# Layer 0's value sums in eights, a fourth weight buffer, and an earlier end of a pass, in a two-layer attention and expert kernel

## Chip, core and metric

The kernel runs on one core of a Trainium2 chip, in one launch. The metric is the device time of that core in microseconds (us). Engines are named as the profile names them: PE is the matrix engine (TensorE), PEld its weight loads, DVE the vector engine, ACT the scalar engine, POOL is GpSimd, and SP only issues transfers. PSUM is the memory that PE writes its results to, SBUF the working memory.

## What is computed

There are 16 sequences of 512 tokens with 128 features, all float32, and two layers. What matters here is cut out of the reference:

```python
# both layers, 16 heads of 8 features, B = 16 sequences, S = 512 tokens
scores = einsum('bhqd,bhkd->bhqk', q, k) / sqrt(8)      # layer 1: causal, keys after the query at -inf
attn   = softmax(scores, axis=-1)
ctx    = einsum('bhqk,bhkd->bhqd', attn, v)

# layer 0: x + memory(xn) + block(xn)
#   memory: a test-time-trained two-layer MLP, updated by gradient steps over 8 chunks of 64 tokens (a scan)
#   block:  convolution, attention as above once, layernorm, 8 dense experts of width 512, layernorm
# layer 1: x + attn1(xn) + moe(xn)
#   attn1:  q,k,v; causal attention; a convolution of its result gives new queries; causal attention
#           again with the same k,v
#   moe:    a router takes 8 of 32 experts a token (128 places each), small MLPs, weighted sum
```

So each sequence has one attention without a mask in layer 0 and two causal ones in layer 1.

## The kernel before

**Turns.** Everything is written as Python generators ("stages") that the class `Turns` steps in turns: in every turn each live stage is stepped once, in the order of its priority number, and what it emits goes into the program. PE executes in exactly this order (it is under a manual schedule), so the order of stages in a turn is the order of PE's work. The other engines' orders are made by the framework's scheduler, in part bound by `issue_after`. A stage that is added to `turns.stages` with the current turn's number joins in the next turn.

**One attention pass.** The 16 heads are done in two halves (c = 0 and 1), a pass each. A pass has two parts. `largest` (priority 0) computes scores and takes row maxima on DVE; `weighted` (priority 1) later computes the transposed scores again with the maxima folded in, 64 rows deep in two halves of the array (float32r), takes the exponential on ACT into a tile `e` (L470), and multiplies `e` with the values into PSUM tile `pc` (L196, 128 rows deep, 32 columns wide, four heads beside each other in the array). One step of `weighted` is called a look; one turn has at most one look of `largest` and one of `weighted`. In layer 0 a pass has 16 looks of two heads over 512 queries. In layer 1 the mask cuts it to 11: four looks 512 wide, four 384 wide, two 256 wide (four heads each), and one 128 wide with eight heads. There POOL zeroes the masked triangle of `e` with two selects per look (L474), after the exponential and before the value product.

**The value products lag.** Finished heads wait in a list `old`. In a later look, behind that look's scores on PE, `tail(pools["heads"])` sums heads in groups of four, at most two groups at once, and only if the list holds at least `pools["heads"]`. That number is 4 in the first part of the program and 8 from the start of layer 1's work on. What is left at the end of a pass is done by the stage `summed` (priority 2): value products, the copy `cs` of `pc` to SBUF on ACT (L444), a transpose `tpc`, and the division by the softmax sums on DVE.

```python
        locks.remove("p2")
        free_slots.append(slot)
        turns.stages.append((turns.turn, 2, ends(summed(old, tail, last, c, cnv), name)))
```

These lines (L484 to L486) run when `weighted` is stepped once more after its last look, in the turn after it; `summed` itself is first stepped one turn later still. The lock `p2` lets the next pass take its first look in the turn in which it is removed. PSUM holds one score tile of `weighted` at a time (`p2` = 1), so a look's scores wait for the exponential of the look before.

**Buffers.** `e` takes 4 KB of each partition. In the first part all `e` tiles come from three buffers of pool `att`; later they come alternately from three of `att` and three of `mid`. Pool `sm` keeps four buffers of each of its small tiles.

**Around it.** The memory scan (priority 3) shares the first part with layer 0's attention. The dense experts of layer 0, `ffn` (priority 6, PE matmuls `phe` and `pye`, L584 and L594), run as a filler of turns: a balance of estimated PE time decides how many units each turn gets, and with `pools["pairs"]` none go into a turn with value products unless more than three are due. `middle` (priority 4) ends layer 0 and computes layer 1's router: logits `lg`, their eight largest, a mask `lr`, and weights that go with the tokens into `xwt` and to memory. `fill` adds a matmul without use to a turn with little work for the array while the experts do not run.

Of the kernel before, what the change touches and what calls it, by code (L numbers as in the profile page):

```python
# [9 lines left out]
F32 = mybir.dt.float32  # L10
# [4 lines left out]
ALU = mybir.AluOpType  # L15
AX = mybir.AxisListType

P = 128
B, S, D = 16, 512, 128
N = B * S  # L20
TB = S // P
# [6 lines left out]
NT8, NH = 8, 4  # L28
EXP0, DFF = 8, 512

EXP1, FF1, TOPK = 32, 96, 8
# [42 lines left out]
def bc(ap, axis, n):  # L74

    u = ap.unsqueeze(axis)
    shape = list(u.shape)
    shape[axis] = n
    return u.to_broadcast(shape)
# [3 lines left out]
def network(ctx: ExitStack, tc: tile.TileContext, a, out):  # L83
    nc = tc.nc
# [4 lines left out]
    sm = ctx.enter_context(tc.tile_pool(name="sm", bufs=4))  # L89
# [50 lines left out]
    pools, done, locks, clock, newest, cleared, held, read, cell = {}, {}, set(), [0], [None], [None], [0], [0], []  # L140
# [3 lines left out]
    def mark(*m):  # L144
        done[m] = clock[0]
# [27 lines left out]
    def drop():  # L173

        read[0] += 1
# [89 lines left out]
    def ends(stage, name):  # L265
        yield from stage
        mark(*name)
# [155 lines left out]
    def weighted(slot, vp, c, causal, cn, name):  # L423


        q, k, _ = slot
        yield from acquire("p2")
        cnv = cn.rearrange("p t (a c j d) -> p (t a) c j d", c=2, j=2, d=DH)
        old, last = [], []
        got = []  # L430

        def values(heads):
            for head in heads:
                kt, n, t, r, e = head
                lent.discard(id(head))
                g = 2 * (t % 2) + r
                j = t // 2
                mm(
                    got[0][32 * g : 32 * g + 32, S - n :], vp[:, kt, 4 * g + 2 * c + j, :], e,
                    start=(kt == 0 and j == 0), stop=(kt == TB - 1 and j == 1),  # L440
                )
            if kt == TB - 1 and t == NH - 1:
                cs = att.tile([P, S], F32, tag="cs", bufs=1, name="cs")
                nc.scalar.copy(cs, got[0])  # L444
                locks.remove("ctx")
                last.append(cs)

        def tail(least):
            if not got and "ctx" not in locks:
                locks.add("ctx")  # L450
                got.append(pools["ps"].tile([P, 512], F32, tag="ctx", bufs=1, name="pc"))
            if got and len(old) >= least:
                locks.add("values")
                for _ in range(min(len(old) // 4, 2)):
                    values([old.pop(0) for _ in range(4)])

        for i, (kt, n, per, t) in enumerate(widths(causal)):
            while len(old) >= pools["heads"] and not got and "ctx" in locks:
                yield
            s = pools["ps"].tile([P, 2, 512], F32, tag="p2", bufs=pools["p2"], name="s2")  # L460
            sv = s[:, :, 0 : per * n].rearrange("p r (i n) -> p r i n", i=per)
            for u in range(per):
                for r in range(2):
                    rr = slice(64 * r, 64 * r + 64)
                    mm(sv[:, r, u, :], k[rr, t + u, kt * P : (kt + 1) * P], q[rr, t + u, S - n :])
            tail(pools["heads"])

            pool = pools["weights"][i % len(pools["weights"])]
            e = pool.tile([P, 2, 512], F32, tag="e", bufs=3, name="e")
            nc.scalar.activation(e[:, :, 0 : per * n], s[:, :, 0 : per * n], AF.Exp, scale=SCALE)  # L470
            ev = e[:, :, 0 : per * n].rearrange("p r (i n) -> p r i n", i=per)
            if causal:
                for r in range(2):
                    cleared[0] = nc.gpsimd.affine_select(  # L474
                        out=ev[:, r, :, 0:P], in_=ev[:, r, :, 0:P], pattern=[[0, per], [1, P]],
                        compare_op=ALU.is_ge, fill=0.0, base=0, channel_multiplier=-1,
                    )
            for u in range(per):
                for r in range(2):
                    old.append((kt, n, t + u, r, ev[:, r, u, :]))  # L480
                    if pool is pools["mid"]:
                        lent.add(id(old[-1]))
            yield
        locks.remove("p2")  # L484
        free_slots.append(slot)
        turns.stages.append((turns.turn, 2, ends(summed(old, tail, last, c, cnv), name)))  # L486

    def summed(old, tail, last, c, cnv):

        while old:  # L490
            tail(4)
            yield
        cs, = last
        yield from room()
        held[0] += 1
        tp = turn4(lambda t: cs[:, t * P : (t + 1) * P], "tpc")
        yield
        tv = tp.rearrange("p (b j x) -> p b j x", j=2, x=16)
        rec = sm.tile([P, TB * NG, 2], F32, tag="rec", name="rec")
        nc.vector.reciprocal(rec, tv[:, :, :, DH])  # L500
        nc.vector.tensor_tensor(cnv[:, :, c], tv[:, :, :, 0:DH], bc(rec, 3, DH), ALU.mult)
        drop()
        yield
# [135 lines left out]
    att = main.enter_context(tc.tile_pool(name="att", bufs=1))  # L639
    early = main.enter_context(ExitStack())  # L640
    fa = early.enter_context(tc.tile_pool(name="fa", bufs=2, side="right"))
    ff = main.enter_context(tc.tile_pool(name="ff", bufs=1))
    ps = main.enter_context(tc.tile_pool(name="psum", bufs=1, space=PSUM))
    pools.update(ps=ps, p2=1, work=3, weights=[att], mid=None, heads=4, pairs=True)
    Wt = Pack(load(fa, "pb", [P, sum(PB.values())]), PB)
    cell.append(Wt.t)
    row.update(load_rows(fa, "rows0", ROWS0))
# [520 lines left out]
    def middle(mid, b):  # L1168

        yield from after(("ffn", b))  # L1170
        ac = mid.tile([P, TB, D], F32, tag="am", bufs=2, name="am")
        nc.sync.dma_start(flat(ac), x1d[0, b])
        xa = mid.tile([P, TB, D], F32, tag="st", bufs=4, name="xa")
        nc.sync.dma_start(xa, acc_b[b])
        x2 = mid.tile([P, TB, D], F32, tag="st", bufs=4, name="x2")
        yield from idle(2)
        yield from layernorm(x2, ac, row["g2"], row["b2n"])
        nc.gpsimd.tensor_tensor(x2, x2, xa, ALU.add)
        yield from idle(3)
        nc.sync.dma_start(acc_b[b], x2)  # L1180

        xwt = mid.tile([P, TB, XW], F32, tag="xwt", bufs=1, name="xwt")
        xn2 = xwt[:, :, 0:D]
        yield from layernorm(xn2, x2)
        yield from idle(3)
        yield from room()
        xT = mid.tile([P, S], F32, tag="st", bufs=4, name="xT2")
        transpose_tokens(xT, xn2)
        nc.sync.dma_start(xt[1, b], xT)
        mark("x2", b)  # L1190
        yield from idle(2)
        yield from room()
        prl = work("prl")[:, 0 : TB * EXP1].rearrange("p (t e) -> p t e", e=EXP1)
        for t in range(TB):
            mm(prl[:, t, :], xT[:, t * P : (t + 1) * P], D1("gw"))
        lg = sm.tile([P, TB, EXP1], F32, tag="lg", name="lg")
        nc.scalar.copy(lg, prl)
        yield
        t8 = sm.tile([P, TB, TOPK], F32, tag="t8", name="t8")
        lr = sm.tile([P, TB, EXP1], F32, tag="lr", name="lr")  # L1200
        for t in range(TB):
            nc.vector.max(t8[:, t, :], lg[:, t, :])
            nc.vector.match_replace(lr[:, t, :], t8[:, t, :], lg[:, t, :], -BIG)
            if t == 1:
                yield
        yield
        nc.vector.tensor_tensor(lr, lr, lg, ALU.not_equal)
        nc.vector.tensor_tensor(lg, lg, bc(t8[:, :, 0], 2, EXP1), ALU.subtract)
        yield
        nc.scalar.activation(lg, lg, AF.Exp)  # L1210
        yield from room()
        pct = work("pct")[:, 0:P]
        mm(pct, lr.rearrange("p t e -> p (t e)"), row["tri"])
        ct = mid.tile([P, P], F32, tag="st", bufs=4, name="ct")
        nc.scalar.copy(ct, pct)
        for t in range(TB):
            of = ct[EXP1 * t : EXP1 * (t + 1), :]
            nc.sync.dma_start(ctab_v[:, b * TB + t, :], of)
            nc.sync.dma_start(totT[:, b * TB + t : b * TB + t + 1], of[:, P - 1 : P])
        yield  # L1220
        nc.vector.tensor_tensor(lg, lg, lr, ALU.mult)
        sw = sm.tile([P, TB], F32, tag="sw", name="sw")
        nc.vector.tensor_reduce(sw, lg, AX.X, ALU.add)
        nc.vector.reciprocal(sw, sw)
        nc.vector.tensor_tensor(xwt[:, :, D:], lg, bc(sw, 2, EXP1), ALU.mult)
        nc.sync.dma_start(xw_b[b], xwt)
        mark("xw", b)
        yield
# [381 lines left out]
```

## Time and profile before

| | us |
|---|---|
| runs of the kernel | 3680.49, 3687.93, 3685.94; median 3685.94 |
| the profiled execution: time | 3691.89 |
| the profiled execution: span of the profile | 3690.2 |
| PE busy / DVE busy / ACT busy / POOL busy | 3464.8 / 2283.7 / 2156.5 / 1575.3 |
| exponentials (L470, ACT), 1216 of them | 1191.9 |
| value products (`pc`, PE), 6144 records | 639.8 |
| selects (L474, POOL), 1408 of them | 469.6 |

The profile is of one execution, 6 us above the median of the runs. PE writes two records for one float32 matmul[...] and one for a float32r matmul; matmuls overlap, so the distance from a group's start to the start of the next is what the group costs, and the durations in the rows are longer than that. PEclk is the granted share of PE's clock.

By the work that stands in it, the program has four parts in this execution: a start (0 to 100 us), layer 0's attention beside the scan (100 to about 1545 us), layer 1's attention beside the experts (about 1720 to 3110 us, with a passage before it), and an end in which the experts are done and layer 1's last sequences, the routed experts and the sum are left (3110 to 3690 us).

### The profile page before, as it was taken

The numbers are of one execution on the slowest core, as the hardware profiler recorded it, in microseconds if no ns is written. First come the engines' busy times: TensorE is split into PE (matmuls) and PEld (weight loads), VectorE is DVE, ScalarE is ACT, GpSimd is POOL, SyncE is SP. The second block draws the span as 40 slices with busy tenths as digits, with TensorE's granted clock in tenths as the row PEclk, the third lists the DMA queues.
The fourth block names the chain that finished last, engine by engine and source line by source line (L and its number), as shares of the span: only waits on it lengthen the run. The fifth ranks groups of instructions, "written<-read, shape, count | busy, mean of one in ns | idle before, by whom it ended". The sixth has DMA issues, their size and how long they took to land. (4 is left out here: it accounts for less than half of the span.)

```text
span 3690.2 us, 62824 instructions
## 1 busy us (share of the span) xinstructions
PE 3464.8 (94%) x22191; PEld 1928.6 (52%) x22191; DVE 2283.7 (62%) x5907; ACT 2156.5 (58%) x3703; POOL 1575.3 (43%) x2524
## 2 busy tenths in 40 slices
PE   6999999899999899999999999999999999998887
PEld 3445555454555455455555555555555655443443
DVE  5676656566756566556466666666666666777652
ACT  1556656665656687666566666666656665543433
POOL 5433532432441455432444344434443444433665
PEclk7999999899999999999999999999999999997888
DMA  5222222223123242443434443444344433333333
GB/s 171 68 68 74 74 76 72 68 72 85 55 67 94 85 114 88 129 124 104 136 95 134 114 133 99 125 117 133 96 130 125 119 101 110 106 103 94 83 86 90
DMA packets 290075, 370.83 MB, mean 100 GB/s; under 512 B 46017, under 2 KB 141409, under 8 KB 289377
## 3 DMA queue, kind: packets, MB, share of 16 engines
q1 hardware_dynamic: 282592, 359.99, 34.2%
q0 software_dynamic: 7168, 6.82, 1.1%
q8 instruction: 177, 2.90, 0.3%
q14 instruction: 138, 1.12, 0.1%
HBM read 236.85 MB, written 133.25 MB: 100 GB/s over the span
## 5 line engine op out<-in xcount | busy, mean ns | idle before, releaser
L470 ACT ACTIVATE e<-s 128x1024 f32<-128x1024 f32 (+1 forms) x1216 | 1191.9, 980 | 651.0 <-PE s L196 574.3
L399 DVE TENSOR_REDUCE nm<-s 128x1 f32<-128x512 f32 (+2 forms) x1408 | 906.5, 682 | 527.7 <-PE s L196 526.3
L391 DVE CUSTOM_DVE_ANT_0 s<-s,sb_const 128x512 f32<-128x512 f32 (+1 forms) x1024 | 624.2, 643 | 433.8 <-PE s L196 428.1
L474 POOL TENSOR_SCALAR_AFFINE_SELECT e<-e 128x128 f32<-128x128 f32 (+2 forms) x1408 | 469.6, 370 | 859.7 <-ACT e L470 852.9
L196 PE MATMUL s<-kx,qx 64*128 64x512 f32 (+3 forms) x3072 | 660.8, 433 | 59.3 <-DVE nm L399 15.3
L196 PE MATMUL pc<-e,vp 128*32 128x512 f32 (+3 forms) x6144 | 639.8, 508 | 30.6 <-POOL e L474 30.5
L196 PEld LDWEIGHTS s<-kx,qx 64*128 64x128 f32 x3072 | 295.1, 189 | 638.4 <-issue 254.6
L594 PEld LDWEIGHTS pye<-ew,hTe 128*128 128x128 f32 x4096 | 517.7, 192 | 173.9 <-issue 158.6
L196 PE MATMUL s<-qx,kx 64*128 64x512 f32 (+3 forms) x3072 | 535.1, 362 | 39.4 <-ACT e L470 28.3
L594 PE MATMUL pye<-ew,hTe 128*128 128x128 f32 x4096 | 564.6, 281 | 0.8 <-ACT hTe L584 0.8
L196 PE MATMUL phe<-x1T,ew 128*128 128x512 f32 x1024 | 539.8, 611 | 8.4 <-DVE nm L399 6.4
L584 ACT ACTIVATE hTe<-phe,sb_cols 128x512 f32<-128x512 f32 x512 | 353.1, 690 | 280.1 <-PE phe L196 278.0
L196 PEld LDWEIGHTS s<-qx,kx 64*128 64x128 f32 x3072 | 295.3, 190 | 85.1 <-ACT e L470 62.2
L602 POOL TENSOR_TENSOR ac<-ac,y 128x512 f32<-128x512 f32 x128 | 164.7, 1287 | 408.6 <-ACT y L601 380.7
L398 DVE TENSOR_TENSOR s<-s,sb_const 128x256 f32<-128x256 f32 (+1 forms) x384 | 180.9, 516 | 237.0 <-PE s L196 232.8
L196 PEld LDWEIGHTS pc<-e,vp 128*32 128x32 f32 x6144 | 154.3, 111 | 271.1 <-issue 177.4
L196 PEld LDWEIGHTS phe<-x1T,ew 128*128 128x128 f32 x1024 | 157.7, 192 | 59.8 <-issue 34.1
L601 ACT ACTIVATE y<-pye,pr 128x128 f32<-128x128 f32 x512 | 147.3, 369 | 30.8 <-PE pye L594 25.8
L391 DVE DVE_READ_ACCUMULATOR2_ANT nm<- 128x1 f32 x1024 | 144.5, 141 | 0.0
L203 PE MATMUL fill<-sb_pd,sb_const 128*128 128x512 f32 (+2 forms) x234 | 118.8, 595 | 0.2 <-DVE lo L330 0.2
L209 POOL TENSOR_SCALAR rs_t<-ss 128x4 f32<-128x4 f32 (+1 forms) x56 | 12.0, 214 | 239.6 <-ACT sq L262 238.4
L209 POOL TENSOR_SCALAR rs_t<-ln_mv 128x4 f32<-128x4 f32 x64 | 12.8, 200 | 178.3 <-DVE ln_mv L219 176.0
(294 smaller groups left out, 3898.8 us busy)
## 6 DMA issues: line engine op xcount, KB each, us to landing
ew<-in_ew SPq DMA_DIRECT2D x256, 256.0 KB
kx<-rk SPq DMA_DIRECT2D x192, 256.0 KB
qx<-rq SPq DMA_DIRECT2D x128, 256.0 KB
rq<-hi SPq DMA_DIRECT2D x64, 256.0 KB
rq<-lo SPq DMA_DIRECT2D x64, 256.0 KB
rk<-hi SPq DMA_DIRECT2D x64, 256.0 KB
rk<-lo SPq DMA_DIRECT2D x64, 256.0 KB
qx<-r SPq DMA_DIRECT2D x64, 256.0 KB
```

Of the source, the lines that this page charges most:

```text
L196: nc.tensor.matmul(o, lhsT=lhsT, rhs=rhs, start=start, stop=stop)
L203: nc.tensor.matmul(o[:, 0:n], lhsT=ident, rhs=cell[0][:, 0:n], start=True, stop=True)
L209: nc.gpsimd.tensor_scalar(t, src, scale, eps, ALU.mult, ALU.add)
L391: newest[0] = nc.vector.tensor_tensor_reduce(out=sv[r][:, 0, :], in0=sv[r][:, 0, :], in1=row["caus"][:, S - n :], scale=1.0, scalar=-BIG, ...
L398: nc.vector.tensor_tensor(dg, dg, bc(row["caus"][:, S - P :], 1, per), ALU.add)
L399: newest[0] = nc.vector.tensor_reduce(nm[:, qt, r, t : t + per], sv[r], AX.X, ALU.max)
L470: nc.scalar.activation(e[:, :, 0 : per * n], s[:, :, 0 : per * n], AF.Exp, scale=SCALE)
L474: cleared[0] = nc.gpsimd.affine_select(out=ev[:, r, :, 0:P], in_=ev[:, r, :, 0:P], pattern=[[0, per], [1, P]], compare_op=ALU.is_ge, fill= ...
L584: nc.scalar.activation(hs[i], ph, AF.Relu, bias=col("fb", i))
L594: nc.tensor.matmul(pye[0][:, t, :], lhsT=h[:, t * P : (t + 1) * P], rhs=w2[e][:, f, :], start=(f == 0 and t == 0), stop=(f == 3), skip_gro ...
L601: nc.scalar.mul(y[:, t, :], pye[0][:, t, :], pr[:, t, e : e + 1])
L602: nc.gpsimd.tensor_tensor(ac, ac, y, ALU.add)
```

## The change

Layer 0's passes also wait for eight heads (`heads=8`), so `pc` gets two groups of four at once. The four looks that then wait need four `e` tiles: the fourth look of every four takes its tile from a new single buffer in pool `fa`. The room comes from the router's tables: `lg` lives in the part of `xwt` that its result goes to in any case, and `lr` in pool `mid` with one buffer in place of four. And `weighted` adds the stage `summed` in the turn of its last look, so it is first stepped in the next turn, one turn earlier than before. This holds for every pass of both layers.

```diff
@@ weighted
             pool = pools["weights"][i % len(pools["weights"])]
-            e = pool.tile([P, 2, 512], F32, tag="e", bufs=3, name="e")
+            e = pool.tile([P, 2, 512], F32, tag="e", bufs=1 if pool is fa else 3, name="e")
             nc.scalar.activation(e[:, :, 0 : per * n], s[:, :, 0 : per * n], AF.Exp, scale=SCALE)
...
+            if kt == TB - 1 and t + per == NH:
+                turns.stages.append((turns.turn, 2, ends(summed(old, tail, last, c, cnv), name)))
             yield
         locks.remove("p2")
         free_slots.append(slot)
-        turns.stages.append((turns.turn, 2, ends(summed(old, tail, last, c, cnv), name)))
@@ network
-    pools.update(ps=ps, p2=1, work=3, weights=[att], mid=None, heads=4, pairs=True)
+    pools.update(ps=ps, p2=1, work=3, weights=[att, att, att, fa], mid=None, heads=8, pairs=True)
@@ middle
-        lg = sm.tile([P, TB, EXP1], F32, tag="lg", name="lg")
+        lg = xwt[:, :, D:]
         nc.scalar.copy(lg, prl)
...
-        lr = sm.tile([P, TB, EXP1], F32, tag="lr", name="lr")
+        lr = mid.tile([P, TB, EXP1], F32, tag="lr", bufs=1, name="lr")
...
-        nc.vector.tensor_tensor(xwt[:, :, D:], lg, bc(sw, 2, EXP1), ALU.mult)
+        nc.vector.tensor_tensor(lg, lg, bc(sw, 2, EXP1), ALU.mult)
         nc.sync.dma_start(xw_b[b], xwt)
```

## The prediction, made before the changed kernel ran

> **What bounds the kernel now.** I read the page first, then busy time by stretches, then PE's timeline in each stretch, then the waits.
>
> ```profile
> span 3690.2 us, 62824 instructions
> PE   6999999899999899999999999999999999998887
> PEclk7999999899999999999999999999999999997888
> ...
> 100.00:1545.00 1445.00, 1362.79 (x7840) 738.44 (x7840) 903.39 (x1635) 928.75 (x1808) 579.35 (x558) 0.98 0.28 81
> 1720.00:3110.00 1390.00, 1367.61 (x9916) 817.75 (x9914) 854.15 (x2634) 860.19 (x1380) 592.37 (x1265) 1.00 0.41 117
> 3110.00:3400.00 290.00, 262.85 (x1704) 125.64 (x1701) 218.46 (x665) 132.66 (x166) 115.91 (x285) 0.89 0.36 97
> ```
>
> The columns of the last three lines are length, then busy us of PE, PEld, DVE, ACT and POOL, then clock. Beside the experts (1720 to 3110) PE is busy 98% at full clock: whatever PE does or waits for there is paid in full. Beside the scan it is 94%, with 82 us of gaps. In the end part it is 91% and less, fills included, and DVE is at 75%: nothing bounds alone. So I count what the change does to PE, stretch by stretch, the layer-1 passes too, since the third edit is theirs as well.
>
> **Fewer entries into the value products: -15.6 us.** The part with four heads at a time, then the part with eight, where layer 0's last passes already run so:
>
> ```profile
> 779.60 1.07 PE L196 MATMUL pc<-e,vp 128*32 128x512 f32 x8
> 780.59 0.50 PE L196 MATMUL s<-kx,qx 64*128 64x512 f32 x2
> ...
> 1581.53 1.92 PE L196 MATMUL pc<-e,vp 128*32 128x512 f32 x16
> 1583.38 0.50 PE L196 MATMUL s<-kx,qx 64*128 64x512 f32 x2
> ```
>
> Start to next start is 0.996 us for four heads (8 records) and 1.854 for eight (read to the ns), so two visits cost 1.992 and one 1.854: 0.138 saved. It is the same whether scores or a full-array matmul follow. In PE's built order 226 visits of four and 79 of eight (512 wide) become 192 of eight: 113 fewer, x 0.138 = -15.6 us. This is a certain term: the rows of both forms are in this trace, in a stretch where PE bounds.
>
> **What the new spacing does to the turns beside the scan: +4 us.** I sorted that stretch's turns by what the program puts on PE. Beside the visits, three classes change. Turns with a fill rise from 13 to 17; a fill after scores costs 1.056 us to the next start: +4. Turns with nothing but the two looks rise from 6 to 10; such a turn takes 1.28 us (one exponential plus its hand-over) where PE's work is 0.57: +3. Turns with four expert units fall from 20 to 12 and those with two rise; a four-unit turn has 0.38 us of gaps on average, a two-unit turn 0.02: -3.
>
> **The fourth buffer: 0.** With four tiles for four waiting looks, every fourth exponential must wait until the first group of four heads has been summed, about 0.95 us after the scores; before, it had a free tile. What covers it: PE itself is in the 1.854 us of value products. The exponential (1.025 us) then ends about 2.36 us after its scores began; the next scores cannot begin before 0.327 + 1.854 + 0.337 = 2.52 us. Margin 0.16. Behind it on ACT stand experts' relus and scan copies, and no expert units run in a turn with values. If the cover is gone, an ACT operation of 0.6 us slipped in between costs 0.44 us; in a third of some 115 turns that is 17 us. A gain is excluded, as no tile comes free earlier. I take 0, the row nearest being eights with scores behind them, which run on without a gap (above).
>
> **The router's tables: 0.** The same instructions at the same sizes, once per sequence; a table is needed again 44 turns later, so one buffer is enough, and they neither add nor move a DMA.
>
> **The earlier end of a pass.** In layer 0 it is free: the next pass's first scores wait for the last exponential in any case, and no select stands behind it. In layer 1 it is not. Here is a pass's end beside the experts, before the change:
>
> ```profile
> 2219.43 0.56 PE L196 MATMUL s<-qx,kx 64*128 64x128 f32 x8
> 2219.91 1.07 PE L196 MATMUL pc<-e,vp 128*32 128x256 f32 x16
> 2220.11 1.02 ACT L470 ACTIVATE e<-s 128x1024 f32<-128x1024 f32 x1
> 2220.91 0.44 PE L196 MATMUL s<-kx,qx 64*128 64x384 f32 x2
> 2221.19 0.50 PE L196 MATMUL s<-qx,kx 64*128 64x512 f32 x2
> 2221.20 1.23 POOL L474 TENSOR_SCALAR_AFFINE_SELECT e<-e 128x512 f32<-128x512 f32 x2 [3.72 <-ACT e L470]
> 2221.62 1.16 PE L594 MATMUL pye<-ew,hTe 128*128 128x128 f32 x8
> ...
> 2223.91 0.40 PE L196 MATMUL s<-qx,kx 64*128 64x512 f32 x2
> 2224.24 0.64 PE L196 MATMUL pc<-e,vp 128*32 128x128 f32 x16
> ```
>
> Line 1 is the last look (eight heads, 128 wide), line 3 its exponential, line 6 its two selects, which end at 2222.43. Line 5 is the next pass's first look. The last value products come a turn later, at 2224.24, with experts' work (2221.62) in between. In the changed order they stand directly behind line 5, in the next pass's first turn: PE reaches them at 2221.19 + 0.33 = 2221.52 and must wait until 2222.43, 0.91 us. PE executes in order, so experts' units, projections and the next turn's looks wait behind them. Reading all 44 passes of 1720 to 3110 us this way, the last select ends after that place in 37, by 0.65 to 2.43 us and 40.6 in sum, 1.10 each; over 0.9 is POOL being late with other work. In the changed order, 29 of the 44 passes of the experts' part have nothing else in between: 29 x 1.10 = 32. Ten have a value projection (`pv`) there, 1 us of PE work that nearly covers the wait: 1 in all. Five have something small: 2. Together **+35 us**, and PE's gaps of that stretch are only 22 us in all, so little of it can be given back. The end part has 20 passes, 13 without cover: 14 us, of which I take half, as DVE, fills and the routed experts set part of those turns: **+7**.
>
> The waits view says that this hand-over is tight already, with the slack of a turn that most groups have:
>
> ```profile
> PEld pc L196 <- POOL e L474: 60.2, 78, 5.5
> PE pc L196 <- POOL e L474: 30.5, 26, 4.6
> ```
>
> On the other side, results leave a pass one turn earlier, and the program ends after 1276 turns in place of 1279. The last turns are latency, not work; at some 2 us each (between the 1.28 of a bare turn and the 2.65 mean of the end part) that is **-6**.
>
> **A rule about the clock.** Do these stalls also cost clock? Beside the scan a gap of 1.27 us is followed by a half-rate slice:
>
> ```profile
> 1478.38 1.03 PE L196 MATMUL pgt<-sb_gw,x1T 128*128 128x8 f32 x8 [1.27 <-DMA x1T<-x1d]
> ...
> 1479.70:1483.10 3.40, 3.40 (x14) 0.70 (x10) 1.76 (x5) 0.89 (x1) 0.17 (x1) 0.50 0.68 224
> ```
>
> The Trainium skill ("TensorE: Matmul & The Clock Gate", Part 1: The HAM clock gate) says that PE falls to half rate after at least one idle window of about 3.4 us. By that rule the stalls cost no clock: 0. By this row, each of the 11 stalls over 1.3 us could cost half of a 3.4 us slice: 11 x 1.7 = 19. Nearest are the stretch's own rows: seven gaps over 0.9 us stand in 1720 to 3110, and the granted clock there is 1.00. I take 0 and keep 19 for the range.
>
> **Sum.** -15.6 + 4 + 0 + 35 + 7 - 6 = +24 us. Against the profiled execution's time of 3691.9 this gives 3716; it lies 6 us above the median, and I carry the difference to the median of 3685.9: 3710 (+0.7%).
>
> **The rivals.**
> *Faster: the wait at a pass's end is covered.* Place: the first turn after a layer-1 pass. The rest of the sum is -18, spread over some 50 exposed passes, so below 0.36 us a pass the change gains. That needs PE to arrive later, behind work that the scheduler's new order makes late anyway (a late exponential holds scores and values alike), or to regain the stall in later gaps. Against it: PE stands at 98%, and in 37 of 44 passes the selects were later than the place. If 10 of the 42 us remain, -8; if none, -18: 3668 to 3678. A better fall of the 82 us of gaps beside the scan could do the same, since ACT's order is made anew.
> *Much slower: the exponential's wait is not covered either.* Then ACT is late in layer 0's turns, scores wait (one score tile), and 17 us come on top, with up to 19 of clock: 3726 to 3740. For: a margin of 0.16 us. Against: ACT is busy only 64% there.
> *No change by cancelling.* If a third of the stalls is regained and the gaps beside the scan shrink a little, the terms meet within 0.2%.
> *The change does not do what it says.* Excluded: the built order shows 192 visits of eight, and the last products directly behind the next pass's first look.
>
> **The numbers.** My forecast, 3697 to 3726: 0.52. Much slower: 0.14. No change: 0.12. Faster: 0.22. About 0.2% (7 us) is what a measurement of this kernel can tell from no change. So slower 0.66, same 0.12, faster 0.22. The range runs from 3669, inside the faster case, to 3732, inside the much slower one; the forecast's own range is 3697 to 3726.
>
> **What would show it.** Right: 16-record `pc` groups alone in the scan's stretch, at 1.85 us, that stretch about 12 us shorter; the waits `pc` <- POOL `e` L474, 91 us on PE and PEld now, up by 35 or more, at the 128-wide form; the counterpart of 1720 to 3110 longer, PE's share there 2 points lower. Wrong: 128-wide groups without a gap before them, or scores <- ACT `e` grown beside the scan.

## The result, and the profile after

| | before | after |
|---|---|---|
| median of the comparison's runs, us | 3686.93 (3680.49 to 3692.67) | 3736.7 (3731.53 to 3741.88) |
| ratio, with its 95% interval | | 1.0133 [1.0113, 1.0153] |
| the profiled execution: time, span | 3691.89, 3690.2 | 3731.53, 3729.8 |

The change makes the kernel slower by 1.3%. The sign was predicted, the size was not: +50 us between the medians in place of +24, and outside the range of 3669 to 3732. The profiled executions lie 39.6 us apart, since the one of before is slower than its median and the one of after the fastest of its four; the parts below add up to these 39.6.

The first two stretches of the prediction, in after (columns: length, busy us of PE, PEld, DVE, ACT, POOL, clock, DMA share, GB/s):

```profile
100.00:1545.00 1445.00, 1374.95 (x7975) 756.67 (x7976) 914.08 (x1668) 938.93 (x1825) 592.05 (x573) 0.99 0.28 82
1720.00:3110.00 1390.00, 1335.24 (x9507) 791.11 (x9508) 839.64 (x2543) 827.17 (x1326) 570.94 (x1219) 0.99 0.40 115
```

In equal windows PE got through 135 more records beside the scan and 409 fewer beside the experts, where its share fell from 98.4% to 96.1%. Fixed windows mix work, though. For a bookkeeping I cut both executions at the same work instead: at the first, fourth, thirteenth and fourteenth sequence's router (`prl`). PE's timeline of before, then of after, these four starts:

```profile
1597.71 1.08 PE L196 MATMUL prl<-sb_pd,xT 128*128 128x32 f32 x8
1922.41 0.98 PE L196 MATMUL prl<-sb_pd,xT 128*128 128x32 f32 x8
3024.50 0.98 PE L196 MATMUL prl<-sb_pd,xT 128*128 128x32 f32 x8
3142.22 0.98 PE L196 MATMUL prl<-sb_pd,xT 128*128 128x32 f32 x8
```
```profile
1577.06 1.08 PE L196 MATMUL prl<-sb_pd,xT 128*128 128x32 f32 x8
1918.98 0.98 PE L196 MATMUL prl<-sb_pd,xT 128*128 128x32 f32 x8
3069.99 0.98 PE L196 MATMUL prl<-sb_pd,xT 128*128 128x32 f32 x8
3186.32 0.98 PE L196 MATMUL prl<-sb_pd,xT 128*128 128x32 f32 x8
```

| part | before | after | difference | PE idle | granted half its clock |
|---|---|---|---|---|---|
| scan part: to the first router | 1597.7 | 1577.1 | -20.7 | 116.5 to 104.0 | 116.1 to 75.1 |
| start of layer 1: first to fourth router | 324.7 | 341.9 | +17.2 | 8.6 to 15.3 | 3.4 to 10.2 |
| steady part: fourth to thirteenth, 9 sequences | 1102.1 | 1151.0 | +48.9 | 15.7 to 43.5 | 0 to 34.1 |
| one more sequence | 117.7 | 116.3 | -1.4 | 4.4 to 7.1 | 10.2 to 3.4 |
| end: from the fourteenth | 548.0 | 543.5 | -4.5 | 80.3 to 88.9 | 131.8 to 96.4 |

All are us. As an estimate, work at half clock (granted 0.50) takes twice its time, so half of what PE was busy in such a stretch is lost. So the gain beside the scan is there and larger than predicted, but much of it is clock; the start of layer 1 takes it back; and the steady part loses 5.4 us a sequence.

Beside the scan, eights run alone, at 1206.81 to 1208.66 = 1.85 us:

```profile
1206.81 1.92 PE L196 MATMUL pc<-e,vp 128*32 128x512 f32 x16
1208.66 1.16 PE L196 MATMUL pj<-sb_pa,xTr 128*128 128x128 f32 x8
```

Beside the experts, the pass's end became what the prediction described. The timeline of after, PE with ACT and POOL:

```profile
1969.95 0.56 PE L196 MATMUL s<-qx,kx 64*128 64x128 f32 x8
1970.43 1.07 PE L196 MATMUL pc<-e,vp 128*32 128x256 f32 x16
1970.63 1.02 ACT L470 ACTIVATE e<-s 128x1024 f32<-128x1024 f32 x1 [0.89 <-POOL ac L603]
...
1971.71 0.50 PE L196 MATMUL s<-qx,kx 64*128 64x512 f32 x2
1971.73 1.22 POOL L474 TENSOR_SCALAR_AFFINE_SELECT e<-e 128x512 f32<-128x512 f32 x2 [1.15 <-ACT e L470]
...
1972.42 0.41 PE L196 MATMUL pc<-e,vp 128*32 128x128 f32 x2 [0.21 <-POOL e L474]
...
1973.00 0.64 PE L196 MATMUL pc<-e,vp 128*32 128x128 f32 x14 [0.18 <-POOL e L474]
...
1973.57 1.13 PE L196 MATMUL phe<-x1T,ew 128*128 128x512 f32 x2
```

The last products start after the first select and wait again for the second. The idle times in brackets (0.21 and 0.18) understate the stall, because a group's duration in the rows runs past the point where the next could have started: from the next pass's first look to the work behind the products it is 1973.57 - 1971.71 = 1.86 us, where the quickest such pair of look and products in before takes 0.89. Summed that way over the 44 passes of the experts' part, the stall is 7.8 us before and 40.5 after, so **+32.7**. The waits of after:

```profile
PEld pc L196 <- POOL e L474: 107.8, 154, 6.1
ACT e L470 <- PE pc L196: 104.0, 86, 2.6
PEld s L196 <- ACT e L470: 103.7, 149, 3.6
PE pc L196 <- POOL e L474: 58.5, 93, 5.7
PE s L196 <- ACT e L470: 28.6, 41, 3.3
```

The select's wait (first and fourth line) went from 90.7 to 166.3. The second line is the exponential that waits for the fourth buffer: 24.8 before. Lines 3 and 5, scores waiting for the exponential, were 102.1 and 28.3 before; in the scan part alone PE's share of it is 15.4 before and 17.0 after. So the wait is there on ACT, and its cover holds.

Two things appear that the prediction had not in its sum. First, layer 1's projection waits for a transfer; the groups of the tile `pjq`, "idle until" (us, times), of which before has no such line:

```profile
its engine sat idle before it (us, times) until:
  DMA xT<-xt: 19.6, 11
```

13.0 of these 19.6 us fall in the steady part, in seven waits. SP's queue at one of them, first before, then after; then PE in after, with the 3.41 us behind the wait:

```profile
2040.66 0.34 SPq L1237 DMA_DIRECT2D xT<-xt  x1
2051.87 0.50 SPq L416 DMA_DIRECT2D top<-m  x1
```
```profile
2040.14 0.34 SPq L1190 DMA_DIRECT2D xt<-xT  x1
2040.58 0.38 SPq L521 DMA_DIRECT2D ew<-in_ew  x1
2050.33 0.50 SPq L416 DMA_DIRECT2D top<-m  x1
2052.59 0.33 SPq L517 DMA_DIRECT2D ew<-in_ew  x1
2053.02 0.39 SPq L1238 DMA_DIRECT2D xT<-xt  x1
```
```profile
2056.03 1.62 PE L196 MATMUL pjq<-xT,sb_pd 128*128 128x512 f32 x2 [1.97 <-DMA xT<-xt]
...
2056.50:2059.91 3.41, 3.41 (x9) 1.50 (x8) 1.50 (x5) 1.89 (x4) 0.22 (x1) 0.50 0.00 0
```

Before, the load of `xT` stands ahead of `top<-m` in SP's queue. In after it follows its store `xt` by 12.9 us, because `top<-m` and a weight load stand ahead of it and are waiting themselves. In the nine steady sequences the load is issued 10.0 to 13.9 us after the store and PE starts the projection 3.0 to 3.6 us later, on arrival. Before it was issued 2.4 to 9.6 us after the store and 11.0 to 18.5 ahead of the projection. Second, PE is granted half its clock (0.50 in the last line) in ten such slices of 3.41 us in the steady part, 34.1 us, where before has none. Each of the five waits for `xT` of 1.97 us and more has one within 1.6 us behind it; the other five slices have no PE gap over 1.28 us in the 7 us ahead of them.

### The profile page after: what moved, and what is told of

It is laid out like the page before. It is cut to its first block, busy times and chain, and to the rows that moved or that the text cites. A ratio compares the mean times of both kernels' runs of the same rounds, so it can differ in the third digit from the quotient of the medians.

```text
span 3729.8 us, 62808 instructions
## 1 busy us (share of the span) xinstructions
PE 3470.9 (93%) x22205; PEld 1943.1 (52%) x22205; DVE 2297.8 (62%) x5907; ACT 2157.1 (58%) x3703; POOL 1573.6 (42%) x2524
## 3 DMA queue, kind: packets, MB, share of 16 engines
q1 hardware_dynamic: 282592, 359.99, 33.4%
## 5 line engine op out<-in xcount | busy, mean ns | idle before, releaser
L196 PE MATMUL pc<-e,vp 128*32 128x512 f32 (+3 forms) x6144 | 621.5, 500 | 59.5 <-POOL e L474 58.5
L196 PEld LDWEIGHTS pc<-e,vp 128*32 128x32 f32 x6144 | 171.5, 110 | 335.4 <-issue 201.7
L444 ACT COPY cs<-pc 128x512 f32<-128x512 f32 x96 | 56.0, 583 | 48.2 <-PE pc L196 46.3
```

What stands on the lines that cost most here:

```text
L196: nc.tensor.matmul(o, lhsT=lhsT, rhs=rhs, start=start, stop=stop)
```

## The experiments

Where a time stands beside "steady", it is the steady part of the table above, in the one profiled execution of that kernel; idle and half-clock times are of that execution too. Each of the ratios is of all its runs, to the kernel before on the same chip; the change has 1.0133.

**The early end, by layers.** First, after with the early end in layer 0 alone:

```diff
-            if kt == TB - 1 and t + per == NH:
+            if not causal and kt == TB - 1 and t + per == NH:
...
         free_slots.append(slot)
+        if causal:
+            turns.stages.append((turns.turn, 2, ends(summed(old, tail, last, c, cnv), name)))
```

> The changed kernel with the earlier end of a pass for layer 0's passes alone; layer 1's passes end as in the kernel before. My theory: the change is a gain of about 20 us beside the scan (fewer entries into the value products) and a loss of about 65 beside the experts that the earlier end brings alone. Then this kernel needs neither the stall before the 128-wide value products nor any other loss: 3687 - 20 = 3667 us, between 3660 and 3674. Rival: the loss comes from the eights, the fourth buffer or the moved tables (ACT's order, exponentials that wait for PE); then the loss stays, 3710 or more.

Measured: 3694.95, ratio 1.0017 [1.0006, 1.0028]; steady 1107. The other half, before with the early end in layer 1 alone:

```diff
+            if causal and kt == TB - 1 and t + per == NH:
+                turns.stages.append((turns.turn, 2, ends(summed(old, tail, last, c, cnv), name)))
             yield
         locks.remove("p2")
         free_slots.append(slot)
-        turns.stages.append((turns.turn, 2, ends(summed(old, tail, last, c, cnv), name)))
+        if not causal:
+            turns.stages.append((turns.turn, 2, ends(summed(old, tail, last, c, cnv), name)))
```

> The kernel before with one edit: layer 1's passes end a turn earlier; fours, three weight buffers and the tables as before. My theory: the whole loss and no gain, 3687 + 65 = 3752 us less what the end part regains (about 5), so 3740 to 3760, with waits of the 128-wide value products on POOL (some 33 us) and of the projection pjq on the DMA of xT. Rival: the loss needs the eights of layer 0 too; then under 3715.

Measured: 3761.48, ratio 1.0187 [1.0164, 1.0210]; steady 1152, stall 41.0 us, 19.0 us of waits for `xT`. So the loss of the steady part comes from layer 1's early end (1152 with it alone), and next to none of it from the eights (1107 with them, 1102 before). But my 3667 for the first kernel fell: its scan part is short (1579), yet the start of layer 1 takes 345 us in place of 325, and the gain is gone.

**The select.** The last look's selects are left out of after:

```diff
-            if causal:
+            if causal and kt < TB - 1:
```

> The changed kernel without the two selects of layer 1's last looks (their masked triangles are not zeroed, so layer 1's attention is not the reference's). The order of PE is the same. If the select stall is what I measured (33 us beside the experts, up to 17 in the end part, of which a half counts), 3695 to 3708. If other waits take its place, as in e3, 3720 or more. The waits of pjq on xT should stay.

Measured: 3707.99, ratio 1.0044 [1.0029, 1.0059]: 0.9% of the 1.3% go with this one wait, some 33 us of the whole kernel. The waits fall to the level of before:

```profile
PEld pc L196 <- POOL e L474: 57.1, 79, 4.6
...
PE pc L196 <- POOL e L474: 26.4, 27, 3.3
```

Steady is 1131, not 1102: half-rate time is still 34 us and the waits for `xT` still 16.

**The transfer: more turns, more work, or another order.** A lag of three turns for the projections in after (`after(("x2", b), lag=3)` in `front1`):

> The changed kernel; layer 1's front stage starts three turns behind the turn in which its input was written to memory, the distance that it had in the kernel before, where it waited for a value buffer that the earlier end now frees two turns sooner. My theory: the projection pjq waits for the DMA of xT (19.6 us in 11 sequences) and each wait is followed by a half-rate slice of PE; without them the kernel is 25 to 35 us faster than the changed one, 3702 to 3712, near what I had forecast. Rival: the loss over the forecast is the select stall itself, larger than sized, and the waits on xT only take the place of other waits; then 3730 or more.

Measured: 3757.51, ratio 1.0179 [1.0159, 1.0199]. The steady waits for `xT` are gone, but steady is 1142 with 8 groups of `phe` and 7 of `pye` fewer in it than in after, which is 13 us of work put off (a group costs 0.87 and 0.90 us to the next start). PE's idle time is 48.8 us where after has 43.5: among others `tpc` waits now,

```profile
2445.47 0.63 PE L248 MATMUL tpc<-sb_const,cs 128*128 128x128 f32 x4 [1.30 <-DVE nm L399]
```

and the end takes 572 us in place of 544, with three waits of 5.5 us for the same transfer there. The lag with no last select, in sequences before the 14th:

> As e6 (last selects left out), and layer 1's front stage three turns behind its input's way to memory for sequences 0 to 12. If select stall and xT wait together are the loss of the steady part beside the experts (5.4 us per sequence more than before), the router's distance from sequence 3 to 12 is that of the kernel before, 1102 us against 1151, and the time 3680 to 3697. If the late transfer only changes places with another wait, no faster than e6.

Measured: 3699.26, ratio 1.0020 [1.0007, 1.0034], steady 1122. The time is below that of either edit alone, but the stretch again lacks the same 13 us of work: at equal work it is no shorter than without the selects alone (1131). The start of layer 1 is 8 us shorter here than there (332 against 340). Two matmuls without use ahead of the projection:

```diff
+            if n == "q" and 0 < b < 13:
+                for _ in range(2):
+                    nc.tensor.matmul(pj, lhsT=ident, rhs=D1.t[:, 0:512], start=True, stop=True)
```

> The changed kernel with two matmuls without use (512 columns, 0.85 us each) directly ahead of pjq in sequences 1 to 12, in the time in which PE stands there. The wait on xT stays, only idle time is filled. Theory that the idle time also costs clock: the half-rate slices behind pjq go, and the kernel is 8 to 15 us faster than the changed one, about 3725, although it does more. Rival, that an idle time of 2 us costs no clock of itself: same time as the changed kernel or a few us more, 3736 to 3742.

Measured: 3743.19, ratio 1.0142 [1.0124, 1.0160], steady 1150 with about 15 us of work added: PE's gaps fell from 43.5 to 33.4 us and half-rate time from 34.1 to 20.5. That it cost almost nothing is a hint that the gap costs more than itself, no more. Then SP's order: `top<-m` told to issue after the last `xT` load (kept in `loaded`).

```diff
+        with ExitStack() as behind:
+            if causal and loaded:
+                behind.enter_context(tc.issue_after(loaded[0].ins))
+            nc.sync.dma_start(at, m.bitcast(F32))
```

> This is the changed kernel, with top<-m of layer 1 told to issue after the last xT load, so that SP issues the load first. PE's order is unchanged. Theory A (SP's queue): the load is issued 3 to 5 us after its store, the projection no longer waits, the 13 us of the steady stretch go (1151 to about 1138), and if these 2 us waits are what sets off the half-rate slices (34 us at half rate), up to another 10: 1125 to 1140, and a time 11 to 25 us below the changed kernel's 3737: 3712 to 3726, ratio 1.006 to 1.010. Theory B (the wait takes another's place): top<-m is late instead, layer 1's scores wait for qx, and the stretch stays at 1145 to 1155, the time within 5 us of 3737.

Measured: 3741.9, ratio 1.0149 [1.0126, 1.0172], steady 1152. The edit did only part of what I meant. In four of nine sequences the load now follows its store by 2 to 4 us, and those have no wait; in five it stands behind the next obstacle, a weight load that waits for its buffer, and is as late as ever:

```profile
2038.21 0.47 SPq L526 DMA_DIRECT2D ew<-in_ew  x1
2050.22 0.33 SPq L522 DMA_DIRECT2D ew<-in_ew  x1
2050.64 0.39 SPq L1243 DMA_DIRECT2D xT<-xt  x1
```

The same order without the last select:

> The same order on SP, and the last look's selects left out as well (the masked triangle of a pass's last look is not zeroed). So both things that PE newly waits for are gone from the earlier end. Theory A: the steady stretch comes down to what it was before the change, 1100 to 1112, half-rate time below 10 us, and the time to 3685 to 3697, of which what is over 3690 is the start of layer 1's part. Theory B: some of the loss is neither, the stretch stays above 1118 and the time above 3700.

Measured: 3701.26, ratio 1.0046 [1.0029, 1.0063], steady 1129: no better than the selects alone. Last, the transfer itself taken away in sequences 3 to 12: the projections read the router's tile.

```diff
+        if 2 < b < 13:
+            xT = kept[b]
+        else:
+            xT = l1.tile([P, S], F32, tag="st", bufs=2, name="xT")
+            nc.sync.dma_start(xT, xt[1, b])
```

> This is the changed kernel, but in sequences 3 to 12 layer 1's projections read the tile xT from SBUF where the router's part wrote it, and not a copy that SP loads back from memory; everything else is in the same order. Theory A (the transfer on SP's queue): the projection's waits of 13 us in the steady stretch go, and half-rate slices with them. The stretch goes from 1151 to 1125 to 1138 and the time to 3712 to 3726. Theory B (something else is late at that place in any case): another wait takes its place, and the time is within 5 us of 3737.

Measured: 3723.54, ratio 1.0083 [1.0066, 1.0100]; steady 1132. The stall at the selects is untouched (13.8 us of gaps at 128-wide products, as in after), the wait is gone, and half-rate time falls from 34.1 to 10.2. So late transfers that PE waited 13 us for cost 19 in the stretch and half a per cent of the kernel. That they took the clock along fits the five slices directly behind them, 17 us at half rate; it is one execution's reading. Both taken away:

> The same, and the last look's selects left out as well (the masked triangle of a pass's last look is not zeroed). Both things that PE newly waits for are gone. Theory A: the steady stretch is back near the 1102 us of the kernel before, at 1100 to 1114, with little half-rate time, and the time is 3685 to 3698, what is over 3690 being the start of layer 1's part. Theory B: something else of the earlier end costs as well, and the stretch stays above 1118.

Measured: 3697.12, ratio 1.0010 [0.9997, 1.0023]; steady 1122. The time is in theory A's range, the stretch is not. PE's gaps are down to 23.6 us (15.7 before), but half-rate time is back at 30.7, which at half speed is 15 us: gaps and clock together account for the 20 us. What sets off these slices with gaps this small was not found, and they speak against the transfer as the only thing that moves the clock.

**The place in the turn.** In after, units of the experts may share the turn of a layer-1 pass's last products (no lock `values` from `summed`):

> The changed kernel; experts' units may go into the turn of a layer-1 pass's last value products (behind them). In the changed kernel two turns in a row, the last look's and the next, get no units unless more than three are due, and half-rate slices stand where PE waited some 2 us in thin turns. If the missing units beside are a cause of their own, half-rate time beside the experts falls from 48 us towards 14 and the kernel gains 10 to 20 us on the changed one (3717 to 3727 on its scale of 3737, ratio to before 1.008 to 1.011). If the stall itself and the xT wait are all, the ratio stays 1.012 to 1.015.

Measured: 3749.04, ratio 1.0143 [1.0128, 1.0157], steady 1162 with 34.1 us at half rate: no help. PE still meets the products first. In the next kernel they come behind the units, in the same early turn:

```diff
-                turns.stages.append((turns.turn, 2, ends(summed(old, tail, last, c, cnv), name)))
+                turns.stages.append((turns.turn, 7 if causal else 2, ends(summed(old, tail, last, c, cnv, not causal), name)))
```

This kernel's attention in layer 1 is not the reference's, and why was not found; its time is read for PE's order alone.

> The changed kernel with the same early turn for a pass's end in layer 1, but its value products last in that turn, behind experts' units that may go there. PE then has about 2 us of units to do while the selects run. If the place in the turn is what costs, the select stall is gone (steady part under 1125 us against 1151) and the ratio is 1.000 to 1.007, with the xT waits left. If the earlier turn itself costs (passes closer together, waits elsewhere), 1.010 or more.

Measured: 3706.95, ratio 1.0044 [1.0027, 1.0062]. This kernel's timeline at a pass's end, PE and the two selects; nothing on PE waits, since the second select ends at 1733.84:

```profile
1732.05 0.40 PE L196 MATMUL s<-qx,kx 64*128 64x512 f32 x2
1732.37 1.13 PE L196 MATMUL phe<-x1T,ew 128*128 128x512 f32 x2
1732.62 1.22 POOL L475 TENSOR_SCALAR_AFFINE_SELECT e<-e 128x512 f32<-128x512 f32 x2
1733.33 1.05 PE L596 MATMUL pye<-ew,hTe 128*128 128x128 f32 x8
1734.32 0.65 PE L196 MATMUL pc<-e,vp 128*32 128x128 f32 x16
1734.89 0.44 PE L196 MATMUL s<-kx,qx 64*128 64x384 f32 x2
```

In the steady part 128-wide products wait 0.3 us in all, the projections not at all (their load is 8.6 to 16.2 us ahead), no slice is at half rate, and gaps are 15.7 us, as before the change. Steady is 1124, but with 26 more `phe` and 128 more `pye` records in it than before, work that the next sequence then lacks (106 us in place of 118): 13 groups of 0.87 us and 16 of 0.90, about 26 us; at equal work it would be some 1098. So the steady part's loss is not in the earlier turn as such. It is in PE meeting the products ahead of the units; that the late transfers and the slices follow from this is likely, as both are gone here too, but not shown by itself.

**Tables, and the start of layer 1.** Before with the tables moved and nothing else:

> The kernel before with the router's tables moved and nothing else. With layer 0's edits alone (e1) the stretch around layer 1's start is 21 us longer than before, although no pass of layer 1 ends earlier there. Theory T: the tables do it (one buffer, writes into the tile that goes to memory); then 3700 to 3710 here. Theory O: it is the new order of the other engines and transfers at that place; then 3683 to 3695, as before.

Measured: 3689.56, ratio 0.9992 [0.9981, 1.0003]: free, and the start takes 325 us as before. The first kernel above with the start of layer 1's turns shifted by one (`t0 = 481`):

> e1 (eights and the earlier end for layer 0 alone) with all of layer 1's stages one turn later. If e1's 21 us around layer 1's start are a matter of how the orders meet there, this loses them or keeps them by chance of the order, and with them gone it is 3670 to 3678, faster than the kernel before. If they come from the eights themselves, 3692 or more again.

Measured: 3698.72, ratio 1.0008 [0.9995, 1.0022]: start 350, steady 1096. The loss at the start stays. The early end only for passes that begin beside the scan:

```diff
+        soon = pools["mid"] is None and not causal
...
-            if kt == TB - 1 and t + per == NH:
+            if soon and kt == TB - 1 and t + per == NH:
...
+        if not soon:
+            turns.stages.append((turns.turn, 2, ends(summed(old, tail, last, c, cnv), name)))
```

> Eights with four buffers, and the earlier end only for passes that begin beside the scan; all passes after it end as in the kernel before. In e1 the stretch from the router's first to its fourth sequence was 21 us longer than before; this kernel differs from e1 only by the ends of layer 0's last passes there. If those ends cost it, the stretch is back at 324 to 330 us, the 16 us beside the scan remain and the ratio is 0.995 to 0.998. If it is a shift of one turn between the layers (the scan ends at turn 496 in place of 497), it stays 340 or more and the ratio is 1.000 to 1.003.

Measured: 3697.33, ratio 1.0012 [1.0001, 1.0023]; scan part 1582, start 342. Against before, PE's gaps in the start are 17.6 us for 8.6 and its half-rate time 17.1 for 3.4: 9 us, and half of 13.7, which is 16 of the loss of 17. The largest gap is again SP's queue, a weight load behind eight small table transfers (the first and last of them shown) and six others; the kernel with the first edit of this part has the same wait (4.24 us):

```profile
1809.58 0.40 SPq L1222 DMA_DIRECT2D ctab<-ct  x1
...
1813.66 0.51 SPq L1223 DMA_DIRECT2D totT<-ct  x1
...
1817.15 0.45 SPq L520 DMA_DIRECT2D ew<-in_ew  x1
...
1823.71 2.05 PE L196 MATMUL phe<-x1T,ew 128*128 128x512 f32 x2 [4.42 <-DMA ew<-in_ew]
```

These table transfers are given to ACT's queue in three sequences:

```diff
-            nc.sync.dma_start(ctab_v[:, b * TB + t, :], of)
-            nc.sync.dma_start(totT[:, b * TB + t : b * TB + t + 1], of[:, P - 1 : P])
+            queue = nc.scalar if b < 3 else nc.sync
+            queue.dma_start(ctab_v[:, b * TB + t, :], of)
+            queue.dma_start(totT[:, b * TB + t : b * TB + t + 1], of[:, P - 1 : P])
```

> This is the kernel with eights and the early end beside the scan alone (the one before this in the document, 3697 us), and the router's four pairs of small table transfers (ctab, totT) of sequences 0 to 2 are issued from ACT's queue in place of SP's. In that kernel's trace the stretch from the first to the fourth router takes 341 us where the kernel before takes 324, with 9 us more of PE gaps and 14 us more of half-rate clock; the largest gap is 4.42 us, phe waiting for the weights ew, whose transfer SP issued at 1817.15, behind eight of these table transfers issued from 1809.58 to 1814.74. Theory A: this queue is where the stretch's loss comes from. Then that wait shrinks below 1 us, a half-rate slice or two go with it, the stretch takes about 333 us, and the time is about 3690, ratio to the kernel before 0.998 to 1.000. Theory B: the loss is a shift of many small waits between the engines, which turns up elsewhere if one is removed. Then the stretch stays at 338 to 345 us and the time at 3694 to 3700.

Measured: 3690.14, ratio 1.0001 [0.9991, 1.0012]. The wait is gone (0.54 us at that place, as before the change), and another of the same size stands earlier, at the exponential. ACT's timeline, and PE's:

```profile
1595.54 0.36 ACTq L1223 DMA_DIRECT2D ctab<-ct  x1
...
1599.61 0.51 ACTq L1224 DMA_DIRECT2D totT<-ct  x1
1600.17 1.02 ACT L471 ACTIVATE e<-s 128x1024 f32<-128x1024 f32 x1 [4.66 <-DMA ctab<-ct]
```
```profile
1601.25 0.80 PE L196 MATMUL s<-qx,kx 64*128 64x512 f32 x2 [3.40 <-ACT e L471]
```

The start still takes 340 us, as theory B has it, while the time is the one of theory A. But this wait is the edit's own: ACT issues the eight transfers one after the other and comes to the exponential 4.66 us late, and again in the next sequence (2.68 us on PE at 1685.46). So the run exchanges one wait for two others and does not show whether the loss of the start lies in SP's queue. No version was faster than the kernel before.

## Why the prediction was right and where it failed

**Fewer entries into the value products, and the turns beside the scan (-15.6 + 4):** the first saving is there: up to the first router the value products take 14.9 us less, start to next start, at full clock. The sum is right only by luck. Kernels with eights reach the first router at 1576 to 1587 us (mean of fifteen 1582), those with fours at 1596 to 1602 (mean of three 1599): -17, where -12 was said. But they also have less time at half clock ahead of it, 65 to 106 us in place of 109 to 126. By the estimate from PE's busy time in these slices that is 11 us of the 17, and in the pair of profiles above 15 of the 21. What is left, some 6, is half of what was said: PE idles 12 us less in that pair, and against the 14.9 the scores cost 12 us more, start to next start, and the fills 5 where 4 was said. Why the clock is better with eights is not shown.

**The fourth buffer (0):** right, for the reason given. ACT's wait rose from 24.8 to 104.0 us, and beside the scan scores wait 1.6 us longer on PE. **The tables (0):** right, by the experiment above.

**The stall at the selects (+35):** right as a count, 32.7 by the same reading; as time it is less. Over the whole kernel the stall so counted is 70 us in after and 20 before, and 12 where the last selects are left out. Those 58 us less are worth 27 to 38 us of time (three pairs of kernels that differ in nothing else). So a good part of the stall so counted does not come out as time, which the prediction allowed for in the end part only.

**The end (+7 and -6):** the sum of the two is right, which the one pair of profiles (-4.5) does not show well, since after has 35 us less at half clock there. The end takes 547 to 556 us in the kernels without layer 1's early end (mean of six 550) and 544 to 555 with it (mean of six 549; the lag of three turns and the order behind the units are left aside). What each term was by itself is not shown. The stall there did double, from 12.5 to 29.7 us.

**The failed step is "The earlier end of a pass", which counted one wait.** The prediction reads every queue that an edit moves work past on PE, POOL and ACT, and never SP's. In after the load of `xT` comes behind transfers that themselves wait, and the slack of 11 to 18.5 us that it had ahead of the projection is gone. That was worth 13 us of waiting, and 19 us of the stretch when it was taken away.

**The other failed step is the choice "I take 0 and keep 19" for the clock.** The trace was closer than the rule of the Trainium skill ("TensorE: Matmul & The Clock Gate", Part 1: The HAM clock gate), which asks for an idle window of about 3.4 us: after has ten half-rate slices in the steady part, and no gap there is longer than 3.1 us. They are 34.1 us, some 17 us of lost work. That this is near the 19 is in part luck, as half of the slices stand behind waits for the transfer, of which the 19 knew nothing. I went by the clock of 1.00 between 1720 and 3110 us before, whose gaps are all under 1.5 us, and overlooked that a longer one lies 19 us outside that window. Before, timeline and window:

```profile
1698.72 0.47 PE L196 MATMUL s<-kx,qx 64*128 64x512 f32 x1 [0.90 <-DVE mp L406]
1701.22 0.50 PE L196 MATMUL s<-kx,qx 64*128 64x512 f32 x1 [2.03 <-DMA kx<-rk]
...
1701.50:1704.91 3.41, 3.41 (x13) 2.32 (x11) 0.76 (x2) 1.02 (x1) 0.00 (x0) 0.50 0.12 28
```

**The start of layer 1 (+17) was in no term.** The kernel with eights and early ends only beside the scan has it in full; tables alone do not bring it. There it is 9 us of PE's gaps, 4.4 of them one weight load behind others in SP's queue, and 7 of clock. Why the gain of the scan part is given back there almost to the microsecond stays open.

So the +24 missed the steady part and the start, not the stall. The start is +17, for which the sum had no term. Of the steady part's 49 us, taking away selects and transfer together returns 29, less than the 20 and 19 that each returns alone; the last 20 are 8 of PE's gaps and some 15 of clock, and their cause stays open, but for this: without layer 1's early end (1107) most of them are not there. Of the rivals, "much slower" had its time about right and its mechanism wrong: it put the clock behind an uncovered exponential, and it came behind the stalls and a transfer.

## What to carry to other kernels

When an edit moves a step by a turn, list what each queue issues around it, the transfer queue first: a load behind a transfer that waits is as late as that one, and a pause counted in turns says nothing of it. An edit that moves transfers to another engine's queue moves their issue time there too. Price a wait of PE of some 2 us at more than its length if the trace shows a lower clock behind such a wait, and look for such rows outside the window too. And cut the two executions at the same work, not at the same time, with idle time and clock beside each part, before adding up: only then did a gain of 21 us, its loss directly behind, and the clock in both become visible.

## What the runs showed of the hardware

Half-rate slices come in multiples of 3.41 us and follow idle of PE shorter than that. In the steady parts of the 18 profiles, 33 of 43 gaps of PE over 1.5 us that begin at full clock have a slice that begins in the gap or within 3.5 us of its end; of 281 gaps between 0.5 and 1.5 us 66 have one, and of 723 between 0.15 and 0.5 us 27. So the length of a gap matters but does not decide, and the gaps in sum do so even less: the kernel without last selects and without the transfer has 23.6 us of gaps and 30.7 us at half rate, the one with selects and without the transfer 35.3 and 10.2. What picks the moments stays open.

Issuing a small transfer occupied its queue for 0.36 to 0.61 us in the run that moved them to ACT: eight of them held ACT from 1595.54 to 1600.12.
